# The opening of a perceiver block on one core: first norm in chunks, TensorE kept at work, another order of folding, another buffer

## Chip, cores and metric

The kernel runs on one core of a Trainium2 chip. The metric is device time in microseconds (us) for one execution; lower is better. Engines are named as in the profile: PE is TensorE's matmul side and PEld its weight load, DVE is VectorE, ACT ScalarE, POOL GpSimd, SP SyncE (which here only issues loads and stores).

## What is computed

There are 16 batch items of 128 rows and 512 columns (x), each with a context of 2048 rows and 512 columns. Three stages follow each other, all in float32:

```python
x = x + xattn(layernorm(x), ctx)      # softmax(h @ ctx.T) @ ctx, no weights, no scale
x = x + attn(layernorm(x), ...)       # 16 heads of 32, causal, rope on half of each head
x = x + ffn(layernorm(x), ...)        # 2 of 8 low-rank experts, chosen from row 0
```

In the second stage q, k and v are made by a projection down to 64 columns for each head and a second one from 64 to 32:

```python
q_lat = (x @ Wq_down).reshape(b, t, H, L)          # H = 16, L = 64; likewise k, v
q_c = jnp.einsum('bthl,ld->bhtd', q_lat, Wq_up_c)  # likewise q_e, k_c, k_e; v with Wv_up
```

The kernel multiplies the two weights of each of q, k and v once, at the start ("folding"), and uses the 512x512 products `w["q"]`, `w["k"]`, `w["v"]` for all batch items.

## The kernel before

**Stages.** Each batch item goes through four Python generators: `score` (first norm, scores against the context, maxima, exponentials, sums), `attend` (weighted sum of the context, first residual, second norm), `inner` (the second stage up to the third norm) and `experts` (the third stage). Each `yield` ends a piece, and `step` runs the next piece of one item. The list of steps from L962 on interleaves items by hand: the opening brings batch 0 and batch 1 on their way, then a loop works on `inner` of item b, `attend` of b+1 and `score` of b+2, and a hand-written order (CLOSING) ends the last two items.

**What sets the order.** Matmuls, TensorE transposes and most loads keep the order of the program on their engine (`keep_in_program_order` in `matmul`, `transpose` and `load`). Other instructions are placed by a planner that estimates when each can start, except those passed to `pinned` (L150), which keep their program order too. `layernorm` pins the statistics and the norm of first norms (names beginning with `1_`); `root` pins its first instruction for `1_0` and `1_1`.

**A norm.** `norm_pieces` gives four pieces: `bn_stats` over 512 columns and `bn_aggr` on DVE, the root on POOL (add epsilon, then the power -0.5), and subtract and multiply on DVE. For batch items 0 and 1 the norm is turned by TensorE (`tensor_pieces`: four 128x128 transposes against `ident` into one PSUM bank, then one ACT copy into `hT`); later items go by a DVE transpose and two DMAs (`send`, `fetch`).

**Scores.** `score` makes for each of four context tiles of 512 rows a bank of 32 matmuls (`psc <- hT, ctxT`): four groups of 128 context rows, each summed over the four column chunks c. A context tile comes turned from memory (`ctxT`, 1 MB, four buffers), in the plan of `load_turned`; the plain context (`ctx`, 1 MB a tile, four buffers) is for `attend`. The tile `hT1_b` has one buffer (tag `hT1`), and the third norm's turned tile `hT3_b` likewise (tag `hT3`).

**Opening loads.** `x_0`, two context tiles, `x_1`, two more, and so on go out on SP's queue (L962 to L971); `ident` goes out first on ACT's queue (L127), the constants `cst` on POOL's (L125), followed there by the memset of `ones` (L129).

**Folding.** `load_weight` brings the halves of q and k into buffers of `ctxT` and those of v into buffers of `ctx` (L982 to L987). `fold_products` multiplies one half of one weight by its second weight into two PSUM banks and copies them; `fold_turned` transposes the products on TensorE and writes them to `w[n]`. The list `halves` (L1005) takes q, k, v in this order, each turned one step after its products. The last half is turned after the transposes of batch 0's second norm; right behind it stand the projections of `inner`: v, then k, then q.

## Time and profile before

| | us |
|---|---|
| median of 3 runs | 815.83 (815.62 to 816.09) |
| the profiled execution | 815.19 |
| its span, first to last instruction | 813.4 |
| PE idle in that span | 16.4 |
| first matmul of the scores starts | 8.13 |
| first matmul of the projections (v of batch 0) starts | 69.45 |

The profile is of one execution. Its page has the busy time of each engine, slices of the span, the DMA queues, the chain of work that ended last, and groups of like instructions; the trace behind it can be asked for the waits of an engine, the order of time in a window, the tiles and the loads. In a row of the order of time stand start, length, engine, line, operation, output <- inputs, shapes and count, and in brackets how long the engine had been idle and what released it. The lines L115, L138, L141 and L146 are the helpers that issue everything, so groups are told apart by their tiles: `psc` is a bank of scores, `av` the weighted context, `tr` a turned norm, `rs` the root of a norm, `st` and `mv` its statistics. Durations of matmuls overlap: 32 matmuls of 275 ns each take far less than 32 times that.

### The profile page before, as it was taken

What the parts mean: (1) busy time and instruction counts of PE and PEld (TensorE: products, weight loads), DVE (VectorE), ACT (ScalarE), POOL (GpSimd) and SP (SyncE); (2) the same over time, 40 slices, a digit from 0 to 9 for tenths busy, and PEclk for the clock granted to TensorE, in tenths of its full rate; (3) what the DMA queues carried; (4) which work ended last, traced back from release to release, by engine and by line L of the source; (5) the groups of instructions that cost most, each with busy time, mean ns of one, the idle gap of its engine ahead of it and who ended that gap; (6) DMA issues with size and microseconds to landing.
All of it is one profiled execution on the core that took longest, in us unless ns stands there. A gap on an engine that the chain in (4) does not pass through costs nothing.

```text
span 813.4 us, 14283 instructions
## 1 busy us (share of the span) xinstructions
PE 797.0 (98%) x5500; PEld 564.9 (69%) x5500; DVE 529.8 (65%) x1231; ACT 259.9 (32%) x769; POOL 146.2 (18%) x213
## 2 busy tenths in 40 slices
PE   6999999999999999999999999999999999999996
PEld 6856675868667686775768677576867757686554
DVE  1444849577583956759396675948668494755885
ACT  1223324133231512424152232414223242322452
POOL 1000101212111121211212121121212112121204
PEclk9999999999999999999999999999999999999999
DMA  9988285876939588594967859496794948754102
GB/s 374 407 341 347 106 333 221 303 306 192 414 134 344 223 293 340 181 387 150 354 238 268 344 180 389 152 347 262 243 366 167 381 166 313 294 207 195 40 1 77
DMA packets 76867, 211.04 MB, mean 259 GB/s; under 512 B 6400, under 2 KB 42624, under 8 KB 60416
## 3 DMA queue, kind: packets, MB, share of 16 engines
q10 hardware_dynamic: 15696, 113.32, 34.8%
q1 hardware_dynamic: 57168, 84.75, 29.4%
q0 software_dynamic: 3936, 12.07, 4.3%
q8 instruction: 43, 0.70, 0.3%
q14 instruction: 24, 0.20, 0.1%
HBM read 180.23 MB, written 29.88 MB: 258 GB/s over the span
## 4 chain that ended last, share of the span: by engine, by line
PE 95%; DVE 2%; POOL 1%; issue 1%; DMA 0%; ACT 0%; POOLq 0%; DVEq 0%; ACTq 0%
PE psc L138 29%; PE av L138 27%; PE v L138 7%; PE k L138 7%; PE q L138 7%; PE o L138 6%; PE pss_sc L138 2%; PE y L138 2%; PE mid L138 2%; PE ffn L138 2%; PE pss_acc L138 2%; PE tr L141 1%; PE tr_m L141 0%; PE spread L138 0%; PE lg L138 0%
## 5 line engine op out<-in xcount | busy, mean ns | idle before, releaser
L138 PE MATMUL psc<-hT,ctxT 128*128 128x128 f32 x2048 | 237.0, 277 | 1.4 <-ACT hT L115 1.4
L138 PEld LDWEIGHTS psc<-hT,ctxT 128*128 128x128 f32 x2048 | 233.0, 193 | 2.5 <-ACT hT L115 2.0
L138 PE MATMUL av<-ctx,sc 128*128 128x512 f32 x512 | 227.3, 596 | 0.0
L138 PEld LDWEIGHTS av<-ctx,sc 128*128 128x128 f32 x512 | 94.4, 190 | 110.5 <-issue 109.5
L115 ACT ACTIVATE att<-att,nmx 128x128 f32<-128x128 f32 x256 | 98.8, 388 | 84.9 <-DVE nmx L115 84.8
L115 POOL TENSOR_SCALAR rs<-mv 128x1 f32<-128x1 f32 x48 | 10.7, 224 | 435.9 <-DVE g_at L115 209.2
L115 ACT COPY sc<-psc 128x512 f32<-128x512 f32 x64 | 37.5, 586 | 140.0 <-PE psc L138 140.0
L115 ACT ACTIVATE sc<-sc 128x512 f32<-128x512 f32 x64 | 40.2, 630 | 90.9 <-DVE sc L115 90.4
L138 PE MATMUL k<-hT,w_k 128*128 128x128 f32 x512 | 60.1, 275 | 0.0
L138 PE MATMUL q<-hT,w_q 128*128 128x128 f32 x512 | 60.0, 275 | 0.0
L138 PE MATMUL v<-w_v,hT 128*32 128x512 f32 x520 | 59.0, 593 | 0.9 <-DVE w_v L115 0.9
L138 PEld LDWEIGHTS k<-hT,w_k 128*128 128x128 f32 x512 | 58.5, 192 | 1.5 <-issue 0.8
L138 PEld LDWEIGHTS q<-hT,w_q 128*128 128x128 f32 x512 | 58.5, 192 | 0.0
L138 PE MATMUL o<-w_c,yT 128*128 128x512 f32 x128 | 57.8, 594 | 0.0
L115 DVE TENSOR_TENSOR mx<-psc,mx 128x512 f32<-128x512 f32 x32 | 21.6, 675 | 54.9 <-ACT sc L115 54.9
L115 DVE TENSOR_SCALAR h<-x,mv,rs 128x512 f32<-128x512 f32 x48 | 28.2, 587 | 33.3 <-POOL rs L115 33.3
L115 ACT ACTIVATE kb<-kT,cst 128x512 f32<-128x512 f32 (+1 forms) x34 | 36.2, 1112 | 39.7 <-DVE kT L115 39.7
L115 ACT ACTIVATION_READ_ACCUMULATOR att<-att,nmx 128x1 f32 x256 | 47.9, 187 | 0.0
L115 DVE TENSOR_TENSOR sc<-sc,spread 128x512 f32<-128x512 f32 x64 | 42.6, 672 | 3.3 <-PE spread L138 3.3
L115 DVE TENSOR_TENSOR att<-att,rsm 128x512 f32<-128x512 f32 x64 | 43.4, 678 | 0.8
L115 DVE TENSOR_REDUCE nmx<-att 128x4 f32<-128x512 f32 x64 | 41.9, 672 | 0.1
L115 DVE TENSOR_TENSOR mx<-psc,sc 128x512 f32<-128x512 f32 x16 | 11.1, 691 | 46.2 <-ACT sc L115 46.2
(132 smaller groups left out, 849.7 us busy)
## 6 DMA issues: line engine op xcount, KB each, us to landing
ctx<-in_ctx_dram ACTq DMA_DIRECT2D x56, 1024.0 KB, 8.8
ctxT<-in_ctxT_dram ACTq DMA_DIRECT2D x52, 1024.0 KB, 10.5
there_p<-pX SPq DMA_DIRECT2D x28, 512.0 KB, 4.1
pT<-there_p SPq DMA_DIRECT2D x28, 512.0 KB, 4.4
ctxT<-in_ctxT_dram SPq DMA_DIRECT2D x12, 1024.0 KB, 8.4
there<-blocks SPq DMA_DIRECT2D x42, 256.0 KB, 3.2
hT<-there SPq DMA_DIRECT2D x42, 256.0 KB, 2.9
ctx<-in_ctx_dram SPq DMA_DIRECT2D x8, 1024.0 KB, 9.3
```

Source lines behind the costliest of these rows:

```text
L115: ins = issue(*args, **kwargs)
L138: tc.keep_in_program_order(nc.tensor.matmul(*args, **kwargs))
L141: tc.keep_in_program_order(nc.tensor.transpose(*args))
```

## The change

Five things change.

- `ones` are set on POOL before the constants are loaded. `ident` is loaded after the first x, on ACT's queue behind half of it.
- The first x comes in two halves of 256 columns, one on SP's queue and one on ACT's.
- The first norm of batch 0 is a function of its own: statistics of two halves, one aggregate, the root, and then for each chunk of 128 columns a norm on DVE, a transpose on TensorE and a copy on ACT.
- Twelve matmuls of `ones` by `ones` into a bank that nobody reads stand first in TensorE's order.
- The turned first norm of batch 1 is put in the buffer with tag `hT3`. The weights are loaded and folded in the order v, k, q, so v now uses the buffers of `ctxT` and q those of `ctx`.

```diff
+    ones = const.tile([P, P], F32, name="ones")
+    gpsimd.memset(ones, 1.0)
     cst = const.tile([P, C_N], F32, name="cst")
     gpsimd.dma_start(cst, io["consts"])
     ident = const.tile([P, P], F32, name="ident")
-    scalar.dma_start(ident, io["ident"])
-    ones = const.tile([P, P], F32, name="ones")
-    gpsimd.memset(ones, 1.0)
     mhalf = const.tile([P, 1], F32, name="mhalf")
     gpsimd.memset(mhalf, -0.5)
...
             eps = gpsimd.tensor_scalar_add(rstd[:n], mv[:n, 1:2], EPS)
-            if name in ("1_0", "1_1"):
+            if name == "1_1":
                 pinned(eps)
...
-    def load_x(b, queue=nc.sync):
+    def load_x(b):
         xs[b] = p3.tile([P, D], F32, tag="x", name=f"x_{b}")
-        load(xs[b], io["x"][b], queue=queue)
+        if b:
+            load(xs[b], io["x"][b])
+        else:
+
+            for cols, by in ((slice(0, D // 2), nc.sync), (slice(D // 2, D), nc.scalar)):
+                load(xs[b][:, cols], io["x"][b][:, cols], queue=by)
...
+    def first_norm(x, hT):
+
+        stats = const.tile([P, 2, 6], F32, name="st_halves")
+        mv, rstd = const.tile([P, 2], F32, name="mv_first"), const.tile([P, 1], F32, name="rs_first")
+        for half in range(2):
+            vector.bn_stats(stats[:, half], x[:, half * D // 2 : (half + 1) * D // 2])
+        vector.bn_aggr(mv, stats.rearrange("p n s -> p (n s)"))
+        pinned(gpsimd.tensor_scalar_add(rstd, mv[:, 1:2], EPS))
+        gpsimd.tensor_tensor(rstd, rstd, mhalf, ALU.pow)
+        h = p2.tile([P, D], F32, tag="h", name="h_1_0")
+        tr = bank(ps_tr, "tr", "tr_1_0")
+        for c in range(KC):
+            at = slice(c * P, (c + 1) * P)
+            vector.tensor_scalar(
+                mixed(h)[:, c], plain(x)[:, c], mv[:, 0:1], rstd, ALU.subtract, ALU.mult
+            )
+            transpose(tr[:, at], h[:, at], ident)
+            scalar.copy(hT[:, :, c, :], tr[:, at].rearrange("p (a j) -> p a j", a=4))
+
 
     def score(b):
 
-        h = layernorm(xs[b], f"1_{b}", mix=b < 2)
-        yield
-        hT = p1.tile([P, 4, KC, QD], F32, tag="hT1", name=f"hT1_{b}")
-        transposed(h[:], hT, f"1_{b}", b < 2)
+        hT = p1.tile([P, 4, KC, QD], F32, tag="hT1" if b != 1 else "hT3", name=f"hT1_{b}")
+        if b:
+            h = layernorm(xs[b], f"1_{b}", mix=b == 1)
+            yield
+            transposed(h[:], hT, f"1_{b}", b == 1)
+        else:
+            first_norm(xs[b], hT)
+            yield
         yield
...
     load_x(0)
+    scalar.dma_start(ident, io["ident"])
+
+    warm = bank(ps_acc, "acc", "warm")
+    for _ in range(12):
+        matmul(warm[:, :P], ones, ones, start=True, stop=True)
     load_turned(0, [0, 1])
...
-    load_weight("q")
+    load_weight("v")
     load_weight("k")
     step(attend, 0)
     step(score, 0, 2)
     step(score, 1, 2)
-    load_weight("v", "ctx")
+    load_weight("q", "ctx")
...
-    halves = [(i, n, g) for i, n in enumerate(("q", "k", "v")) for g in range(2)]
+    halves = [(i, n, g) for i, n in ((2, "v"), (1, "k"), (0, "q")) for g in range(2)]
...
-            load_x(b + 3, nc.sync)
+            load_x(b + 3)
```

## The prediction

> **What bounds the kernel now.** I read the page's busy table first, then the waits of TensorE, then the order of time of the opening, then the landing times of the loads there, and last the windows at both ends where the TensorE clock can be told.

> ```profile
> span 813.4 us, 14283 instructions
> ...
> PE 797.0 (98%) x5500; PEld 564.9 (69%) x5500; DVE 529.8 (65%) x1231; ACT 259.9 (32%) x769; POOL 146.2 (18%) x213
> ```

> TensorE is idle for only 813.4 - 797.0 = 16.4 us. In windows of its own, it lacks 7.0 us before 8.13, 0.7 up to 30, 1.1 between 54.6 and 73, 0.8 over the 676 us from 110 to 786, and 6.8 in the closing. So the loop over the batches has nothing to win, and every edit here is worth what it does to the first 73 us; a microsecond won there moves everything behind it. The waits of TensorE in the first 100 us name the gaps:

> ```profile
> PE tr L141 <- DVE h L115: 6.3, 1, 6.3
> PE psc L138 <- ACT hT L115: 1.4, 2, 0.7
> PE v L138 <- DVE w_v L115: 0.9, 1, 0.9
> PE tr_fold_k L141 <- ACT folded_k L115: 0.2, 1, 0.2
> ```

> (columns: total us, times, longest). The opening in order of time (start, length, engine, instruction):

> ```profile
> 3.63 0.69 DVE L115 BATCH_NORM_STATS2 st<-x 128x6 f32<-128x512 f32 x1 [3.63 <-DMA x<-in_x_dram]
> ...
> 4.95 0.57 POOL L115 TENSOR_TENSOR rs<-rs,mhalf 128x1 f32<-128x1 f32 x1
> 5.55 0.74 DVE L115 TENSOR_SCALAR h<-x,mv,rs 128x512 f32<-128x512 f32 x1 [1.01 <-POOL rs L115]
> 6.34 0.71 PEld L141 LDWEIGHTS tr<-ident,h 128*128 128x128 f32 x4 [6.34 <-DVE h L115]
> 6.34 1.12 PE L141 MATMUL tr<-ident,h 128*128 128x128 f32 x4 [6.34 <-DVE h L115]
> 7.50 0.59 ACT L115 COPY hT<-tr 128x512 f32<-128x512 f32 x1 [5.04 <-PE tr L141]
> 8.13 12.44 PEld L138 LDWEIGHTS psc<-hT,ctxT 128*128 128x128 f32 x96 [1.08 <-ACT hT L115]
> ...
> 24.87 0.59 ACT L115 COPY hT<-tr 128x512 f32<-128x512 f32 x1 [3.48 <-PE psc L138]
> ...
> 25.51 3.84 PE L138 MATMUL psc<-hT,ctxT 128*128 128x128 f32 x32 [0.74 <-ACT hT L115]
> ```

> A serial chain x, statistics, root, norm, four transposes, one copy ends at 8.13, when the scores begin. At 24.87 the copy of the second batch's turned norm waits for batch 0's last score, since both tiles share one buffer.

> A second cost is no gap. The first score bank runs from 8.13 to 13.65, where its copy starts: 5.5 us for 32 matmuls. The next copies start at 17.23 and 20.80, 3.57 us a bank. The windows (length, then busy us and count of PE, PEld, DVE, ACT, POOL, then clock, DMA share, GB/s) show why:

> ```profile
> 4.79:8.20 3.41, 1.18 (x5) 0.78 (x5) 0.74 (x1) 0.59 (x1) 0.64 (x2) 1.00 1.00 393
> 8.20:11.61 3.41, 3.41 (x16) 3.41 (x17) 0.75 (x2) 0.00 (x0) 0.00 (x0) 1.00 1.02 423
> 800.09:803.50 3.41, 0.95 (x5) 0.33 (x3) 2.58 (x9) 0.29 (x1) 2.96 (x4) 1.00 0.46 135
> 803.50:806.92 3.42, 3.42 (x14) 2.47 (x13) 1.84 (x2) 0.95 (x2) 2.76 (x3) 0.50 0.17 49
> ```

> Until 11.6 a matmul takes 3.41/16 = 213 ns, afterwards 3.57/32 = 112 ns: half clock, although the column still says 1.00 there. The cold stretch costs 5.5 - 3.57 = 1.9 us.

> [...] 8.20 to 11.61 was full and freed it; a window of 0.95 us busy took it away at 803.5, and 1.18 us busy (4.79 to 8.20) didn't free it. The share needed lies between these and a full window. [...] the constants' load was issued by 2.0, yet in the window 3.7 to 5.0 only SP's queue moved bytes. The first turned context tile, issued at 1.18:

> ```profile
> ctxT<-in_ctxT_dram SPq DMA_DIRECT2D x1, 1024.0 KB, 6.3
> ```

> lands at 1.18 + 6.3 = 7.5. That is only 0.65 before its use now, and becomes the limit.

> **Part by part.**

> *First norm in chunks.* Stats of two halves: 0.42 each (the 128x256 rows), 0.05 overlapped, so 0.8 instead of 0.69; x in two halves without ident beside them lands perhaps 0.2 earlier (between 0 and 0.3). The root is unchanged, so the first chunk norm starts at about 5.5. A 128x128 DVE row takes 0.29 (diag), issued some 0.24 apart: chunks end at 5.8, 6.0, 6.25, 6.5. Each transpose takes 0.28 to 0.42, and an ACT copy of 128 columns about 0.25, worked out from the 0.36 and 0.59 of 256 and 512. The last chunk is in place near 7.15 instead of 8.09, and the three before it already feed matmuls. From the norm alone scores could start at about 6.9. But the tile of context lands at 7.5, and its bytes are not moved. ident is now queued behind half of x on ACT's queue, beside SP's megabyte: between 3.9 (its 3.1 from issue) and about 6.2 (if it waits for that tile's packets, as the constants did); in the bad case the transposes end near 6.9 and the copies near 7.6. So I take 7.5 for the start: 0.65 gained, between 0.3 and 1.4 (if the tile lands early too). Eight more small instructions stand on DVE, PE and ACT at a time when nothing else is queued there; half of x on ACT delays its table load by 0.4, needed only at about 6.

> *Ones on TensorE.* ones move ahead of the constants on POOL, ready near 1.5; 12 matmuls at 213 ns run to about 4.1. Nothing real waits for PE then; had they delayed the transposes, each would cost 0.2. 2.6 us is 76% of a window at best and 38% when the phase splits it. Then PE does little until 5.8: an idle window there could take the clock away again. Gain between 0 and 1.9. With a needed share near one third it is nearly all, near one half about 0.75 on average over the phase, near a full window nothing. I take 1.2. The constants start 0.25 later on POOL, first used at 77.5.

> *Own room for the second norm.* The tile goes to the buffer of the third norm, whose first own tenant comes after 100 us. The copy can start as soon as the transposes at 20.6 end, while 3.7 us of scores cover it: the 0.74 gap goes, 0.70 on the chain. What is late next is the context tile behind it: issued 13.65, landed 7.1 later at 20.75, while its use moves from 25.5 to about 22.1. Of the tiles after it the third is tightest: landed 20.79 + 8.2 = 29.0, used at 33.25 now, some 29.8 then. Covered, by 0.8; DMA is at 420 GB/s throughout, so it cannot be hurried.

> *v, k, q.* The same folding matmuls, transposes, copies and loads; only the order and the buffers' names change. Last is now q, needed 7 us after v. After the last transposes at 68.6 PE can start v at once, as hT is copied at 68.2: 0.86 gained. If that cover fails, at most the same 0.86 stays. The wait of 0.2 on folded_k is the second weight's and stays.

> Sum: 0.65 + 1.2 + 0.70 + 0.86 = 3.4. The profiled execution took 815.19, of which 813.4 is span; that gives 811.8. The median shown, 815.83, is 0.64 above it, which gives 812.4. I forecast 812.2, between the two.

> **The rivals.**
> - *The ones don't free the clock* (chance 0.2). For: their 2.6 us never fill a window, and the pause behind them. Against: the true threshold is only known to lie above 35%. Then 2.2 are gained: 813.0 to 813.6.
> - *Everything early* (0.12). ident slips in before the big tile and that tile lands near 6.5[...]; then the start gains 1.3 and the clock 1.9: 811.0 or a bit below.
> - *Loads become the bound* (0.1). The tiles' slack falls to about 0.8 us; if the opening's loads come later through the reordered queues, PE waits on them and 1 to 1.5 of the gain goes: 813.5.
> - *Slower* (0.04). The chunk norms carry no pin, while the second batch's statistics do. If the planner puts these first on DVE, the chunks wait for x of batch 1, landing at 10.8: they start after 11.6 instead of 5.5, scores near 12.9 instead of 8.1, 4.8 lost. Less the 0.9 of v and 1.2 of the clock (the second gap is not there then either, 0.7): 817.8. It decides as soon as that one instruction stands ahead. Against: the planner sees that x come later, and put those statistics behind the first norm before.

> **How the numbers follow.** The forecast has 0.54. Its own bounds are 811.0 to 813.2; with the first three rivals and a half microsecond for the phase of the clock at both ends (the closing has a cold window of its own now, worth about 1), the range is 810.6 to 814.2. A difference of 0.2%, 1.63 us, is about what can be told from none: faster means below 814.2. Slower takes 0.04, within the bound 0.06 (the first and third rivals together), faster the other 0.90.

> **What would show it.** Right: the first score near 7.5 with a wait on the context tile or the copy; the first bank 3.6 to 4.5 us long; no idle before the second batch's first score; v directly behind the last folding transposes; nothing new in the loop. Wrong: a first bank of 5.5 us (clock), transposes waiting on ident past 6.5, waits of scores on ctxT between 11 and 30, or DVE rows of batch 1 ahead of the chunks; or new PE gaps repeated in the loop, which this sum doesn't hold.

## The result and the profile after

| | before | changed |
|---|---|---|
| median of 18 runs each, us | 816.78 (815.50 to 817.47) | 815.29 (813.77 to 817.12) |
| ratio to before, 95% interval | | 0.9985 (0.9978 to 0.9992) |
| span of the profiled execution, us | 813.4 | 813.6 |
| copy of the first score bank starts, us | 13.65 | 15.82 |
| v of batch 0 starts, us | 69.45 | 69.67 |

The change wins about 1.2 us (0.0015 of 816; the interval gives 0.7 to 1.8), where 3.6 were forecast. The two profiles seem to show even less, but the profiled execution of before (815.19) lies 1.6 below the median of the 18 runs and below each of them. The profiled execution of the change took 817.01, of which 3.4 lie outside its span, where most of the others have 1.8. So totals are compared by ratios here, and the profiles are used for what happens at a place.

The waits of TensorE in the first 100 us of the changed kernel (total us, times, longest):

```profile
PE tr L140 <- DMA ident<-in_ident_dram: 2.0, 1, 2.0
PE tr L140 <- ACT hT L115: 1.1, 3, 0.4
PE warm L137 <- POOL ones L115: 1.0, 1, 1.0
PE tr_fold_k L140 <- ACT folded_k L115: 0.2, 1, 0.2
```

The two gaps that the last two edits aimed at, scores on `hT` and v on `w_v`, are gone. Two waits that cost something are new: the first transpose waits for `ident`, and the three others wait for ACT's copies. The opening in order of time shows both:

```profile
0.99 4.38 PE L137 MATMUL warm<-ones 128*128 128x128 f32 x24 [0.99 <-POOL ones L115]
...
5.50 1.17 DVE L115 TENSOR_SCALAR h<-x,mv_first,rs_first 128x128 f32<-128x128 f32 x4 [1.01 <-POOL rs_first L115]
...
7.35 0.38 PE L140 MATMUL tr<-ident,h 128*128 128x128 f32 x1 [1.98 <-DMA ident<-in_ident_dram]
7.77 0.27 ACT L115 COPY hT<-tr 128x128 f32<-128x128 f32 x1 [4.83 <-PE tr L140]
...
8.09 0.48 PE L140 MATMUL tr<-ident,h 128*128 128x128 f32 x1 [0.36 <-ACT hT L115]
...
9.74 0.48 PE L140 MATMUL tr<-ident,h 128*128 128x128 f32 x1 [0.36 <-ACT hT L115]
...
10.01 12.92 PE L137 MATMUL psc<-hT,ctxT 128*128 128x128 f32 x96
...
15.82 0.58 ACT L115 COPY sc<-psc 128x512 f32<-128x512 f32 x1 [5.30 <-PE psc L137]
```

The norm is ready when it was forecast: chunks from 5.50, all four within 1.17 us. But the first transpose starts at 7.35, the others follow in steps of 0.83 us, each after the copy of the one before, and the scores begin at 10.01 instead of 8.13. From the start of the last copy into `hT`, at 10.26, the first bank still takes 5.6 us, so it ran on the low clock although the ones had stood before it. The windows of this execution (length, then busy us and count of PE, PEld, DVE, ACT, POOL, then clock, DMA share, GB/s):

```profile
0.63:4.04 3.41, 3.05 (x14) 3.05 (x15) 0.55 (x2) 1.28 (x1) 1.19 (x4) 1.00 0.60 198
4.04:7.45 3.41, 1.43 (x13) 1.27 (x12) 1.58 (x6) 0.00 (x0) 0.80 (x2) 1.00 1.04 421
7.45:10.87 3.42, 2.35 (x9) 1.50 (x9) 0.47 (x1) 1.06 (x4) 0.00 (x0) 0.50 1.03 424
10.87:14.28 3.41, 3.41 (x17) 3.41 (x17) 1.15 (x3) 0.00 (x0) 0.79 (x2) 0.50 1.01 420
```

The ones keep TensorE busy for 89% of the first window and free the clock for the second (14 rows take 3.05 us before 4.04, the 12 up to 5.37 only 1.33). In that one TensorE is busy for only 1.43 us, and the clock column falls to 0.50 for the next two. The scores start inside these.

Behind the opening nothing new appeared. The window from 110 to 450 us has no idle time at all:

```profile
110.00:450.00 340.00, 340.00 (x2377) 241.75 (x2375) 228.76 (x535) 108.42 (x324) 64.41 (x91) 1.00 0.75 279
```

The gains and losses of the opening can be added up at two places of the two profiles. The fourth score bank of batch 0 starts 2.17 us later than before (23.21 instead of 21.04): the new opening lost that. From there to the weighted values of batch 0's second stage (`y`, 110.96 instead of 110.74) the stretch is 1.95 shorter, which is what the last two edits won. So in the profiles they nearly cancel. The 1.2 us of the medians do not show in them, since the profiled execution of before was faster than all 18 runs.

### The profile page after: what moved, and what is told of

It reads as the page before. It is cut to its first block, busy times and chain, and to the rows that moved or that the text cites. A ratio compares the mean times of both kernels' runs of the same rounds, so it can differ in the third digit from the quotient of the medians.

```text
span 813.6 us, 14339 instructions
## 1 busy us (share of the span) xinstructions
PE 800.7 (98%) x5524; PEld 567.9 (70%) x5524; DVE 530.6 (65%) x1235; ACT 260.4 (32%) x772; POOL 146.9 (18%) x213
## 4 chain that ended last, share of the span: by engine, by line
PE 91%; DVE 3%; DMA 2%; POOL 1%; issue 1%; ACT 0%; ACTq 0%; POOLq 0%; SPq 0%; DVEq 0%
PE psc L137 27%; PE av L137 26%; PE v L137 7%; PE k L137 7%; PE q L137 7%; PE o L137 6%; PE pss_sc L137 2%; PE y L137 2%; PE ffn L137 2%; PE pss_acc L137 2%; PE mid L137 1%; DMA ident<-in_ident_dram 1%; DMA there_p<-pX 1%; DMA x<-in_x_dram 1%; DVE att L115 1%
## 5 line engine op out<-in xcount | busy, mean ns | idle before, releaser
L115 ACT ACTIVATE att<-att,nmx 128x128 f32<-128x128 f32 x256 | 98.8, 388 | 84.6 <-DVE nmx L115 84.6
L115 POOL TENSOR_SCALAR rs<-mv 128x1 f32<-128x1 f32 x47 | 10.5, 224 | 438.8 <-DVE g_at L115 209.2
L115 ACT COPY sc<-psc 128x512 f32<-128x512 f32 x64 | 37.5, 585 | 141.6 <-PE psc L137 141.6
L115 ACT ACTIVATE sc<-sc 128x512 f32<-128x512 f32 x64 | 40.2, 630 | 90.9 <-DVE sc L115 90.4
L115 DVE TENSOR_TENSOR mx<-psc,mx 128x512 f32<-128x512 f32 x32 | 21.6, 676 | 49.9 <-ACT sc L115 49.9
L115 ACT ACTIVATE kb<-kT,cst 128x512 f32<-128x512 f32 (+1 forms) x34 | 36.2, 1112 | 39.7 <-DVE kT L115 39.7
L115 ACT ACTIVATION_READ_ACCUMULATOR att<-att,nmx 128x1 f32 x256 | 47.9, 187 | 0.0
L115 DVE TENSOR_SCALAR h<-x,mv,rs 128x512 f32<-128x512 f32 x47 | 27.4, 583 | 31.1 <-POOL rs L115 31.1
L115 DVE TENSOR_TENSOR mx<-psc,sc 128x512 f32<-128x512 f32 x16 | 11.1, 691 | 54.6 <-ACT sc L115 54.6
L115 DVE TENSOR_TENSOR sc<-sc,spread 128x512 f32<-128x512 f32 x64 | 42.6, 672 | 3.3 <-PE spread L137 3.3
L115 DVE TENSOR_TENSOR att<-att,rsm 128x512 f32<-128x512 f32 x64 | 43.4, 678 | 0.8
L115 DVE TENSOR_REDUCE nmx<-att 128x4 f32<-128x512 f32 x64 | 41.9, 672 | 0.1
## 6 DMA issues: line engine op xcount, KB each, us to landing
ctx<-in_ctx_dram ACTq DMA_DIRECT2D x56, 1024.0 KB
ctxT<-in_ctxT_dram ACTq DMA_DIRECT2D x52, 1024.0 KB
ctxT<-in_ctxT_dram SPq DMA_DIRECT2D x12, 1024.0 KB
ctx<-in_ctx_dram SPq DMA_DIRECT2D x8, 1024.0 KB
```

Source lines behind the costliest of these rows:

```text
L115: ins = issue(*args, **kwargs)
```

## The experiments

Every ratio below is to the kernel before, run on the same chip as the experiment, with its 95% interval. Where two kernels were run on different chips, they are compared by these ratios.

**1. The last two edits together, without the new opening**

```diff
-        hT = p1.tile([P, 4, KC, QD], F32, tag="hT1", name=f"hT1_{b}")
+        hT = p1.tile([P, 4, KC, QD], F32, tag="hT1" if b != 1 else "hT3", name=f"hT1_{b}")
...
-    load_weight("q")
+    load_weight("v")
...
-    load_weight("v", "ctx")
+    load_weight("q", "ctx")
...
-    halves = [(i, n, g) for i, n in enumerate(("q", "k", "v")) for g in range(2)]
+    halves = [(i, n, g) for i, n in ((2, "v"), (1, "k"), (0, "q")) for g in range(2)]
```

> The kernel before with only the second norm's own room and the folding order v, k, q. If these two edits do what their gaps said (0.70 + 0.86 on the chain), the time falls by 1.6 us, ratio 0.998, and the whole gain of the changed kernel is theirs: its new opening then wins nothing. If instead the chain gives the two gaps back later (loads, planner), the ratio is 0.999 to 1.000 and the opening must have won about 1.5 us. In the trace: no PE wait on hT at 25.5 and none on w_v at 69.5, first score still near 8.1.

Measured: 813.41, ratio 0.9963 (0.9950 to 0.9976), about 3.0 us less than before. Neither case fits: the two edits win more than their gaps, and more than the whole change. So the new opening of the change does not merely win nothing; 0.0022 of 816, about 1.8 us (0.6 to 3 with both intervals), is what it costs.

**2 and 3. Each of the two alone.** The first line pair above, and the three others.

> The kernel before with only the second norm's own room. The gap of 0.74 goes; if that is all, 0.7 us less (ratio 0.9991). The trace of room and order together had 0.9 less at this place, since the first bank behind a stall also starts slower: then 0.9 us, ratio 0.9989. If this edit holds most of that run's median gain of 2.9, the ratio is 0.9975 or below.

> The kernel before with only the order v, k, q. By the gap 0.86 us less (0.9989); by the trace of room and order together, where the stretch from the first fold to v was 13.47 instead of 14.83, 1.4 us less (0.9983). The two single edits should add up to that run's ratio of 0.9963; if they fall clearly short of it (product above 0.998), the rest came from the clock's phase or the closing and not from these edits.

Measured: own room 0.9978 (0.9971 to 0.9985), order 0.9990 (0.9982 to 0.9999); their product is 0.9968, inside the interval of the two together. The order does what was said. The room wins twice its gap, and the order of time of TensorE in its trace shows where:

```profile
60.94 1.09 PE L141 MATMUL tr_fold_k<-ident,folded_k 128*128 128x128 f32 x8
61.97 1.09 PE L138 MATMUL fold_v<-down_v,up 64*32 64x512 f32 x16
```

Before, these eight rows stood in two groups:

```profile
61.54 0.66 PE L141 MATMUL tr_fold_k<-ident,folded_k 128*128 128x128 f32 x4
62.43 0.63 PE L141 MATMUL tr_fold_k<-ident,folded_k 128*128 128x128 f32 x4 [0.23 <-ACT folded_k L115]
62.98 1.09 PE L138 MATMUL fold_v<-down_v,up 64*32 64x512 f32 x16
```

There was a wait of 0.23 on the copy of `folded_k` in between, and `fold_v` began 1.44 us after the first of them; now it is 1.03. The order of DVE's instructions shows why. Before, the norm of batch 2 stands ahead of DVE's copy of `folded_k`: DVE idles 1.00 us for that norm's root, and the copy runs from 61.59 to 62.28, just ahead of the second group. With the room alone the copy stands first and fills this pause (59.45). The changed kernel has the old order again, and the wait with it. From the fourth score bank of batch 0 (21.04 before, 21.44 here) to the weighted values of its second stage (`y`, 110.74 and 109.72) the stretch is 1.42 shorter: 0.41 from this wait, and 1.0 at the old gap of 0.74. The additional quarter microsecond there fits the first matmul behind a gap, whose 0.27 (the length of one score matmul in the trace of before, 0.275) no other matmul overlaps; that last reading wasn't tested alone. The same stretch shrinks by 0.96 with the order alone and by 2.36 with both, so the edits add up.

**4. ident first on ACT's queue again, the rest as in the change**

```diff
     ident = const.tile([P, P], F32, name="ident")
+    scalar.dma_start(ident, io["ident"])
...
     load_x(0)
-    scalar.dma_start(ident, io["ident"])
```

> The changed kernel with ident again issued first on ACT's queue, ahead of the second half of x. Theory 1 (ident queued beside the 1 MB tile is what holds the transposes): ident lands near 4, transposes begin near 5.7 instead of 7.35, first score near 8.5 instead of 10.0, 1.6 us less, and more where the clock is no longer taken away in the pause: ratio to before 0.994 to 0.9965. Theory 2 (x in halves and small chunks cost the time): the second half of x now waits behind ident, so nothing is won or 0.3 us lost, ratio 0.9985 to 0.999.

Measured: 817.83, ratio 1.0023 (1.0014 to 1.0031), slower than before and far from both expectations. Now ident is early, and the second half of x has taken its place behind it:

```profile
3.27 0.43 DVE L115 BATCH_NORM_STATS2 st_halves<-x 128x6 f32<-128x256 f32 x1 [3.27 <-DMA x<-in_x_dram]
...
7.17 0.43 DVE L115 BATCH_NORM_STATS2 st_halves<-x 128x6 f32<-128x256 f32 x1 [3.47 <-DMA x<-in_x_dram]
```

The two halves' statistics stood next to each other in the change (0.75 us for both, from 3.49). Here 3.9 us lie between them, and the whole norm waits. So it is not ident that is slow: in every trace where something stands second on ACT's queue here, its first use comes after 7 (from 7.17 in 4 to 8.26 in 5). The traffic of the changed kernel between 3.7 and 5.2 us shows how it went (queue, packets, MB, share of the 16 engines):

```profile
q1 hardware_dynamic: 74, 0.61, 97.9%
q10 hardware_dynamic: 75, 0.04, 8.4%
```

q1 is SP's queue, with the first context tile, and q10 is ACT's, with ident. As many packets of one as of the other were moved, 74 to 75, but SP's have 8 KB and ACT's 512 bytes. Of the 0.64 MB, ident got 0.04. By an estimate from these rows, at 75 packets in 1.5 us ident's 128 rows take 2.6 us. The constants on POOL's queue moved nothing here; these counts don't explain that. In the kernel before, where ident is issued first, it landed 3.1 us after its issue: 125 of the 144 packets that ACT's queue moved in the first 8 us had gone by 3.0, beside 143 of SP's, of 2.3 KB on average. In the change its first use comes 6.2 us after its issue (1.17 to 7.35).

**5. A PSUM bank for each chunk, ident as in the change**

```diff
-        tr = bank(ps_tr, "tr", "tr_1_0")
         for c in range(KC):
             at = slice(c * P, (c + 1) * P)
+            pool, tag = (ps_tr, "tr") if c < 3 else (ps_acc, "acc")
+            tr = bank(pool, tag, f"tr_1_0_{c}")
```

> The changed kernel with a PSUM bank of its own for each of the four chunks' transposes; ident as in the change. Theory 1b (a transpose into a bank waits until the copy of the chunk before it has read that bank): the transposes go in one row from 7.3, no PE wait on the copies, first score near 8.5 instead of 10.0, 1.5 us less, ratio near 0.9965. Rival (the spacing is DVE's or ACT's pace): spacing stays near 0.83 us and the ratio 0.9985.

Measured: 812.38, ratio 0.9949 (0.9936 to 0.9961), 2.9 us less than the change. ident landed even later, and yet:

```profile
8.26 0.63 PE L140 MATMUL tr<-ident,h 128*128 128x128 f32 x4 [1.78 <-DMA ident<-in_ident_dram]
8.60 0.77 ACT L115 COPY hT<-tr 128x128 f32<-128x128 f32 x4 [5.66 <-PE tr L140]
...
8.92 9.31 PE L137 MATMUL psc<-hT,ctxT 128*128 128x128 f32 x81
...
12.79 0.59 ACT L115 COPY sc<-psc 128x512 f32<-128x512 f32 x1 [3.42 <-PE psc L137]
```

The four transposes take 0.63 together, so neither DVE's nor ACT's pace set the steps: the shared bank did. (Each chunk got a tile of its own with its bank; which of the two the waits follow was not told apart.) The scores start 1.1 earlier than in the change, and the first bank takes 3.9 from its first score instead of 5.8. The clock had come at 6.7 in this execution, and the window behind it was 1.81 us busy and kept it:

```profile
6.68:10.09 3.41, 1.81 (x14) 1.60 (x15) 0.00 (x0) 0.77 (x4) 0.00 (x0) 1.00 1.02 420
```

That is partly luck. With the edges of the change's profile (4.04 and 7.45) the ones would have ended at 5.4 and left that window about 1.3 us busy, an estimate from the rows above, and the change lost the clock with 1.43. Two of the five runs have a mean granted clock of only 0.995 and 0.996. Besides, the wait on `folded_k` is gone here too, which is 0.4 of the gain.

**6. Both, 4 and 5**

> Both: ident first and four banks. Theory 1 with 1b: transposes from 5.7, copies done near 7.2, first score bounded by the context tile at 6.3 to 7.5; about 2.6 us less than the change and the clock kept from the ones on in most executions: ratio to before 0.993 to 0.995 (811 to 812.7). If the ones do not keep the clock through the pause of about half a microsecond: ratio near 0.9955. If loads become the bound: PE waits on ctxT between 10 and 30 us appear and the ratio stays above 0.996.

Measured: 815.09, ratio 0.9987 (0.9980 to 0.9993). The statistics of the second half start at 7.37. The four transposes go in a row from 9.51, in 1.25 us and at half clock (0.50 from 8.34 to 11.75), so it is not the clock that removes the steps. x is late as in 4, so the expectation's first step is missing. The banks are worth 0.0036 here too (1.0023 to 0.9987).

**7 and 8. Loads as before, banks, with and without ones.** Experiment 6 with the first x whole on SP's queue, so that ident is alone on ACT's; then the same without the twelve matmuls.

```diff
-        if b:
-            load(xs[b], io["x"][b])
-        else:
-
-            for cols, by in ((slice(0, D // 2), nc.sync), (slice(D // 2, D), nc.scalar)):
-                load(xs[b][:, cols], io["x"][b][:, cols], queue=by)
+        load(xs[b], io["x"][b])
```

> The changed kernel with the loads of before (x whole on SP's queue, ident first on ACT's) and a bank for each chunk. Theory (small loads placed behind another on ACT's queue wait for the 1 MB tile; transposes into one bank wait for copies; the ones keep the clock if the pause behind them is short): x lands near 3.7 and ident near 3.9, transposes near 5.9, scores near 7.3 or when the first context tile lands, clock full from the first bank in most executions: about 2.3 us less than the run with room and order alone, ratio 0.993 to 0.994. If the context tile bounds the start at 8 or later, or the clock falls back all the same: 0.995 to 0.9965.

> The same without the twelve matmuls of ones. If the ones are worth the clock once the pause is short, the first bank is cold again (5.4 us instead of 3.6) and the ratio is 0.9945 to 0.9955, 1.5 us more than with them; if they are worth nothing, it is equal to the run with them within 0.0006.

Measured: 810.73, ratio 0.9941 (0.9927 to 0.9954), and without ones 811.29, 0.9946 (0.9932 to 0.9959). In the traces the first score starts at 7.04 and 7.41, and the first bank's copy at 10.89 and 12.77: 1.9 us apart, 1.5 of it the clock (3.85 and 5.36 from the first score to the copy). The medians differ by 0.6 only, within the intervals. The two traces end 1.4 apart (spans of 808.3 and 809.7). The one with ones has a mean granted clock of 0.998, the other 1.000 (more on this at the end). Where the rest went isn't settled. So what the ones win in the opening is shown by the traces, their worth for the whole run only as somewhere between nothing and 2 us.

**9. Without chunks.** Experiment 1 with the ones: first norm whole, loads as before.

> The kernel before with room, order and the ones, its first norm whole and its loads unchanged. Against old_loads_banks it tells what chunks are worth: the theory gives the chunks 0.4 to 0.8 us, so ratio 0.994 to 0.995 here; against room and order alone (0.9963) it tells what the ones are worth without chunks: 1.0 to 1.9 us. If the ones run into the transposes (they end near 6.4 when cold), nothing is delayed by more than 0.1.

Measured: 810.98, ratio 0.9944 (0.9930 to 0.9957). The first score is at 7.75. Against 1 the ones win about 1.6, with intervals that overlap a little; against 7 the chunks win 0.2 in the medians, 0.7 at the first score, and the intervals overlap. The chunks look like the smallest part of what can be had here.

**10. The change without ones**

> The changed kernel without the twelve matmuls of ones, all else as in the change. Theory: the clock that the ones win is taken back in the pause before 7.4 (a window 42% busy), so the time is that of the change within 0.3 us, ratio 0.998 to 0.999. Rival: the ones save a microsecond or more on average even there, ratio 0.9995 to 1.001. Third: the ones leave the array colder than no ones would, ratio below 0.9975.

Measured: 815.21, ratio 0.9990 (0.9983 to 0.9996), 0.4 us above the change's 0.9985 with overlapping intervals. The ones show no worth where the change has them.

**11. Old loads, one bank**

> The changed kernel with the loads of before, but all four transposes still in one bank. Against old_loads_banks (0.9941) it prices the bank alone when ident is early. Theory: each transpose waits for the copy before it, 0.8 us a step, last copy near 9.0 and scores near 8.9 instead of 7.0, 1.7 us more, and 0 to 1 us for a clock lost on the way: ratio 0.996 to 0.9975. Rival (the bank costs nothing, it was all ident): 0.994 to 0.995.

Measured: 811.23, ratio 0.9946 (0.9932 to 0.9961): better than expected and in the rival's range. The mechanism is there all the same: transposes at 6.34, 7.03, 7.71 and 8.39, each behind a copy, and the first score at 8.56 instead of 7.04. But they take 0.33 instead of 0.48 each, at full clock, and it is kept (the window behind the ones is 2.00 us busy): the first bank takes 3.6 from the last copy. So the shared bank by itself is 1.5 us at this place in the trace, and the ratio shows 0.4 of it, with an interval that holds both 0.4 and 1.5.

**12. Ten ones.** Experiment 7 with ten matmuls instead of twelve.

> old_loads_banks with ten matmuls of ones instead of twelve, as the first transpose there stood behind the last ones (6.27, while its chunk was there at 5.94). If that wait counts, the first score moves from 7.0 to about 6.7 and the time falls by 0.3, ratio near 0.9937; if the context tile or a clock that is released less often decides, the ratio is 0.9941 to 0.995.

Measured: 810.49, ratio 0.9932 (0.9917 to 0.9947), the lowest of all, though not told apart from 7. Its opening:

```profile
0.99 4.56 PE L138 MATMUL warm<-ones 128*128 128x128 f32 x20 [0.99 <-POOL ones L115]
...
6.34 1.10 PE L141 MATMUL tr<-ident,h 128*128 128x128 f32 x4 [0.80 <-DVE h L115]
...
7.28 10.89 PE L138 MATMUL psc<-hT,ctxT 128*128 128x128 f32 x96
...
11.06 0.58 ACT L115 COPY sc<-psc 128x512 f32<-128x512 f32 x1 [3.31 <-PE psc L138]
```

The transposes no longer wait for the ones but for the norm, which came 0.24 later in this execution, so the expected 0.3 at the first score isn't seen.

**13. The change with eighteen ones**

```diff
-    for _ in range(12):
+    for _ in range(18):
```

> The change exactly, but eighteen matmuls of ones instead of twelve, so that TensorE is at work until near 7 and the pause before the transposes is short. ident and the shared bank stay as they are. Theory (the change frees the clock and loses it in the pause): the clock is now kept through the transposes, first score still near 10.0, but its bank takes 3.6 to 4 us instead of 5.6: 1.5 to 1.9 us less than the change, ratio 0.996 to 0.997. Rival A (the copies' waits between the transposes alone are enough to lose the clock): as the change, 0.998 to 0.999. Rival B (where the clock is freed late, the longer row of ones delays the transposes by up to a microsecond and gives it all back): ratio 0.998 to 1.0, with a PE row of ones ending after 7.4.

Measured: 812.21, ratio 0.9945 (0.9931 to 0.9960), 3.3 us less than the change, with intervals that don't meet. Nothing else differs, so six more multiplications of ones that nobody reads are worth some two to four and a half microseconds. The first transpose waits for ident until 8.13 in this trace, and the others for the copies as before; the first score is at 10.32, later than in the change. But:

```profile
2.12:5.53 3.41, 3.41 (x18) 3.41 (x18) 1.03 (x4) 0.82 (x1) 0.96 (x4) 1.00 1.03 384
5.53:8.95 3.42, 2.36 (x19) 1.98 (x18) 1.10 (x4) 0.27 (x1) 0.00 (x0) 1.00 0.98 404
8.95:12.36 3.41, 2.70 (x22) 2.34 (x22) 1.06 (x3) 0.80 (x3) 0.79 (x2) 1.00 1.05 432
```

The window behind the one that freed the clock is 2.36 us busy instead of 1.43, and the clock stays. The first bank's copy starts at 14.10 instead of 15.82. The wait on `folded_k` is gone in this trace as in 5, another 0.4. All five runs have a mean granted clock of 0.998 or more; of the change's 18, two reach 0.998 and thirteen are at 0.995 or below. Two windows at half clock, 6.8 us, take 0.004 off that mean. So, as far as these means tell, the loss in the pause is the rule in the changed kernel, not one execution's bad luck.

## Why the prediction was wrong, step by step

The sign was right and the size was not: 812.2 was forecast from a base of 815.83, and 815.29 was measured against 816.78. The sign was right only because the last two edits won more than the new opening lost; the opening itself, from which 1.85 was expected, went the other way. About 1 us of the miss is the base, since three runs had shown a median that 18 put higher; the rest lies in the opening. "Sum: 0.65 + 1.2 + 0.70 + 0.86 = 3.4" by its terms:

| term | forecast | seen in the traces |
|---|---|---|
| start of the scores | 0.65 earlier | 1.9 later (8.13 to 10.01) |
| clock | 1.2 | nothing: first bank 5.6 instead of 5.5 |
| own room | 0.70 | 1.42 alone, 1.0 of it at the gap; in the change only that 1.0 |
| v, k, q | 0.86 | 0.96 |

- *ident behind x.* The prediction named the wait and bounded it at 6.2, from the constants; the first transpose waited for it until 7.35 in the change and until 8.26 in 5. And it set this beside a context tile that "lands at 7.5" and was to be the limit anyway, so it cost ident at almost nothing. That limit fell: with ident and x early the scores started at 7.04 (7). The 7.5 was one execution's: at 7.04 in 7 and at 7.28 in 12 no score waited for the tile. The reordered queue, not the tile, was the bound. The prediction also took the wait of the constants on POOL's queue for a wait for the tile's packets. They moved nothing from 3.7 to 5.2, when 75 packets of ident's queue went beside the tile's, so they show nothing of the kind.
- *The step that failed outright: "in the bad case the transposes end near 6.9 and the copies near 7.6".* The chunks were priced as a stream on three engines: DVE 0.24 apart, transposes following, copies following. All four transposes write one tile of one bank, and each waits until the copy before it has read that bank. A step of 0.83 us stands in place of 0.25, and this lay in the diff: `tr` is made once, ahead of the loop. In the change's trace the three later transposes stand behind a wait of 0.36 each on the copy before. From the first transpose to the first score the change takes 2.66 us, run 6 with its own banks and the same half clock 1.04. So of the 2.5 us by which the scores missed 7.5, the bank is about 1.6 and ident the other 0.9. "nothing else is queued there" looked for other work, not for the work's own buffer.
- *The ones.* "12 matmuls at 213 ns run to about 4.1" counted rows of the trace as calls. A call leaves two rows (12 calls, 24 rows), and they ran to 5.4. That error helped, by luck: the first window was 89% full and the clock did come, at 4.04. "An idle window there could take the clock away again" was named and valued at a third of the gain; it was the whole, since the late transposes made the pause longer. In the change's profile it was ident's wait that did so: the window that lost the clock ends at 7.45, 0.1 after the first transpose. Run 11, with ident early and the bank still shared, kept the clock (a window with 2.00 us busy). The two errors are tied by this: run 13 buys back the clock with the bank still shared, run 5 the bank and, in its trace, the clock with it. Each wins about 3, of which 0.4 is the wait on `folded_k`.
- *Own room and the order.* Right in mechanism. The room was mis-sized by half, as the fold's 0.2 wait "is the second weight's and stays" was wrong: it went in the run with the room alone and stayed in the change. It follows where the planner puts the norm of batch 2 among DVE's instructions (runs 2 and 3). Why the planner puts it ahead in one kernel and behind in another was not traced.
- *The rivals.* "The ones don't free the clock" came nearest in time (813.0 to 813.6), by another road: they freed it, and it was lost. Loads never became the bound: no wait of scores on a context tile in any trace, even where the first bank's copy starts at 10.89. The slower case did not happen either, as the chunks stand ahead of batch 1's statistics (5.50 and 10.40).

## What to carry to other kernels

When a step is cut in pieces to make a pipeline, give each piece a buffer of its own, or the pieces take turns, as they did here (0.83 us a step, against four transposes in 0.63 in 5); the price is the whole round (write, read, release) for each piece. A small load that is needed early (64 KB here) should be first on its queue, before any large load starts on another one (3.1 us from issue to landing before, 6.2 from issue to use in the change): beside that, it got one small packet for each large one here (75 and 74 in 1.5 us). And keeping TensorE at work for its clock only counts if the row of work nearly reaches the real work (here a window of 1.43 us of work lost the clock, one of 2.36 kept it); the pause is to be measured, and every delay before the real work also lengthens it.
